# Three bf16 parts in place of one fp32 operand in the GRU aggregations of a two-layer graph kernel on one core

## The chip, the core and the metric

The kernel runs on one core of a Trainium2 chip. Five engines work side by side, each through its own queue strictly in the order in which the program lists its instructions: TensorE (PE in the profile, with its weight loads as PEld), VectorE (DVE), ScalarE (ACT), GpSimd (POOL) and SyncE (SP), which here issues all DMAs. Semaphores order the engines among each other. The metric is the device time of one execution in microseconds (us); the median of three runs is compared.

## The reference

128 graphs of 128 nodes with 256 features each, and an adjacency matrix per graph. Layer 0 is a gated graph network of three rounds, layer 1 a graph attention; both take a normalized input and add to it.

```python
h = jnp.maximum(_layernorm(x), 0.0)
A = (adj != 0).astype(x.dtype)
for i in range(3):                                  # layer 0: three GRU rounds
    m = jnp.einsum('bnd,de->bne', h, weight[i])
    aggr = jnp.einsum('bst,bsd->btd', A, m)
    h = _gru_cell(aggr, h, w_ih, w_hh, b_ih, b_hh)  # gates r, z, n
x = x + h
h = jnp.maximum(_layernorm(x), 0.0)                 # layer 1: attention
Wh = jnp.einsum('bnf,of->bno', h, W)
e = leaky_relu((Wh @ a1)[:, :, None] + (Wh @ a2)[:, None, :], 0.2)
att = softmax(where(adj == 0, -inf, e))             # 0 where adj == 0
x = x + jnp.einsum('bij,bjo->bio', att, Wh)
```

All inputs and outputs are fp32; A holds only 0 and 1.

## The kernel before

**Tiles.** Four graphs form a group; there are 32 groups. A group's state exists in two layouts: as columns (`hT`, features on the partitions, 2 chunks by 512 nodes) and as rows (`h`, nodes on the partitions, 4 graphs by 256 features). One *step* is one GRU round of one group, written (group, round); there are 96.

**A step** (`gru_step`). First the aggregation: `inputs` calls `gathered` (L637), which multiplies the rows `h` (the stationary operand, 128x128 per graph and chunk) by A, eight fp32 matmuls of 128 columns into two PSUM banks `pa`; ACT copies them to `aT` (L663), and DVE forms four sums of `aT` (`t_a`, L493, as it has formed `t_h` from `hT`). Then two blocks (`blocks`) of seven products each, a Strassen-like form of the gate matmuls (all at L737, three matmuls of 256 columns per product). Between the products stand evictions that the next product needs: ACT copies bank `u` to `c1_0` (L757) and bank `m7` to `m` (L760); DVE adds `u` and `m` into `c2` (L763), which must be done before the fifth product writes on into `u`; ACT copies `u` to `c1_1` (L770); DVE adds `u` and `m` into `c22` (L774). ACT does the tanh of the gates (L795, L802, L830, L688), DVE the updates: `candidate` (L682) and three passes over 1024 elements that make the new state (L694, L696, L698).

**Rows again.** For nearly every step the new columns become rows by DVE transposes of 32x32 blocks into `tq` and a trip through DRAM (`to_rows_by_blocks`, L590; four DMAs out, four back). Rows live in six buffers `h` (`ROWS = 6`), handed out in turn: rows of the state for a later step, the first rows of a group (`prologue`, `h_a`), and the rows of the attention layer (`epilogue`, `h_b`). A buffer comes free when the matmuls that read it are done.

**The epilogue** of a group, after its third round: rows by way of DRAM, `x1 + h` on DVE (L971), statistics (L440, L442, L446), a power on POOL (L454 to L458), normalization on ACT (L471), eight dot products on DVE (L998), one score vector transposed (L1026), written to DRAM and read back broadcast to all partitions (`line`, then `e`), Prelu on ACT (L1046), the mask `(A-1)*1e30` added on DVE (L930, L1055), row maximum (L1061), exponentials on ACT (L1065), a transpose by way of DRAM (L610), the attention matmuls `pq` (L637 again), `hs` copied by ACT (L1116), `po` (L1124) and the result (L1132).

**What sets the order.** A planner inside the kernel (class `Order`) runs when the program is built. It keeps, for every engine, the time at which it is free, and for every set of buffers ("room") when each comes free. Work beside the products is held in tasks (generators) that ask for an engine, a duration, a time from which they can start and sometimes a room; a task has a rank (0 for aggregation and sums, 0.5 for the new state, 1 for rows and prologue, 2 for the epilogue). `fill` hands out tasks of ACT and DVE while a product runs, the lower rank first when start times are close; `fixed` places an eviction; `finish` runs tasks until given ones are done, whatever PE does in that time. The order that results is fixed in the program, for every engine. The steps follow `plan`, sorted by 3*group + 4*round: in the middle of the run (22,2) is followed by (25,0), (24,1), (23,2) and (26,0). `settle`, called after every product, starts the inputs of the next step; if that step's rows are not yet planned, it calls `order.finish([s.rows])`.

```python
elif not groups[g].due:
    s = groups[g]
    s.due = True
    if s.l == l:
        if s.by_blocks():
            order.finish([s.rows])
        s.task = order.add(0, inputs(s, s.hT_ready))
```

Of the kernel before, what the change touches and what calls it, by code (L numbers as in the profile page):

```python
# [7 lines left out]

F32 = mybir.dt.float32
I32 = mybir.dt.int32  # L10
AF = mybir.ActivationFunctionType
ALU = mybir.AluOpType
AX = mybir.AxisListType

P = 128
D = 256
C = D // P
G = 4
T = G * P
# [8 lines left out]
def preln_gnn_kernel(  # L28
# [49 lines left out]

    ident = const.tile([P, P], F32, name="ident")
    make_identity(nc, ident)  # L80

# [14 lines left out]
            cols = slice(gates.start * D, gates.stop * D)  # L98
            dma(w[k][:, cols], weight[k * P : (k + 1) * P, cols])

    def load_weight(l, pool, shape, tag):
        w = borrowed(pool, shape, tag, f"wt_{l}", C * D)
        w = w.rearrange("p (c d) -> p c d", d=D)
        dma(w, weight_t[l].rearrange("(c p) d -> p c d", p=P))
        wt.append(w)


    load_weight(0, gate, [P, 2, H], "m")
    load_gates(wih, w_ih_t, slice(0, 1))
    xt_0 = io.tile([P, G, D], F32, tag="xt", name="xt_0", bufs=XT)  # L110
    for i in range(0, G, 2):
# [23 lines left out]

    zero = borrowed(gate, [P, C, T], "r", "zero", T, bufs=1).bitcast(mybir.dt.bfloat16)[:, 0:T]
    put(nc.vector.memset(zero, 0.0))
    c1 = [ps_sum.tile([P, 2, H], F32, name=f"c1_{n}") for n in range(2)]  # L140
    c2 = ps_sum.tile([P, 2, H], F32, name="c2")
# [31 lines left out]
    class Order:  # L173
        def __init__(self):
            self.free = dict.fromkeys((PE, ACT, DVE, POOL, SP, "port"), 0.0)
            self.tasks = []

            self.rooms = {room: [0.0] * 2 for room in ("tq", "x1", "prT", "e", "hs")}
            self.rooms |= {"misc": [0.0] * 3, "h": [0.0] * ROWS}
            self.next, self.room_of = dict.fromkeys(self.rooms, 0), {}  # L180

# [36 lines left out]
        def open(self, room, name):  # L218
            self.room_of[name] = room, self.next[room]
            self.next[room] = (self.next[room] + 1) % len(self.rooms[room])  # L220
            if room == "misc" and self.room_of[name][1] > 2:

                return more[self.room_of[name][1] - 3].rearrange("p n t -> p (n t)")
            if room == "misc":
                return ps_misc.tile([P, T], F32, tag="misc", name=name)
            if room == "h":
                return work.tile([P, G, D], F32, tag="h", name=name, bufs=ROWS)
            if room in ("prT", "e"):
                return work.tile([P, G, P], F32, tag=room, name=name)
            if room == "x1":  # L230
                return io.tile([P, G, D], F32, tag="x1", name=name, bufs=2)
            return work.tile([P, C, T], F32, tag=room, name=name)
# [411 lines left out]
            banks.append(pa)  # L644
        return banks, t

    def inputs(s, ready):

        name = f"{s.g}_{s.l}"
        s.tH, s.tA = {}, {}  # L650
        parts = len(s.parts())
        s.hidden = order.add(0, moving_sums(s.hT, s.tH, ready, f"h_{name}", parts))
        if s.l and not s.by_blocks():
            s.h, s.h_ready = yield from rows(s, ready, name)
        banks, ready = yield from gathered(s.h, s.A, s.h_ready, f"pa_{name}")
        order.close(f"h_{name}" if s.l else f"h_a{s.g}", ready)
        aT = None
        for c, pa in enumerate(banks):
            t = yield ACT, 0.57, ready
            order.close(f"pa_{name}_{c}", t)  # L660
            if aT is None:
                aT = columns_tile("aT", name)
            put(nc.scalar.copy(aT[:, c, :], pa))  # L663
        s.aT, s.aT_ready = aT, t
        yield from moving_sums(aT, s.tA, t, f"a_{name}", parts)

    def state_rows(s):
        s.h, s.h_ready = yield from to_rows_by_blocks(s.hT, s.hT_ready, f"{s.g}_{s.l}")

    def flat(tile_, cols):  # L670
        if cols == slice(0, T):
# [12 lines left out]
    def state(s, o, old, new, v, z, cols, graphs, halves, ready):  # L684

        n = v[:, o, cols]
        t = yield ACT, 0.66 if cols == slice(0, T) else 0.47, ready
        put(nc.scalar.activation(n, n, AF.Tanh, bias=bih[:, 2 * C + o : 2 * C + o + 1], scale=1.0))  # L688
        halves.append(t)
        if len(halves) < C:  # L690
            return
        n, new_, z_ = flat(v, cols), flat(new, cols), flat(z, cols)
        t = yield DVE2, both_t(cols), max(halves)
        put(nc.vector.tensor_tensor(new_, flat(old, cols), n, ALU.subtract))  # L694
        t = yield DVE2, both_t(cols), t - HOP
        put(nc.vector.scalar_tensor_tensor(new_, z_, 1.0, new_, ALU.add, ALU.mult))  # L696
        t = yield DVE2, both_t(cols), t - HOP
        put(nc.vector.scalar_tensor_tensor(new_, new_, 0.5, n, ALU.mult, ALU.add))  # L698
        if s.l < NL - 1:
            s.hT, s.aT = new, None  # L700
            s.l += 1
            s.hT_ready = t
            if s.by_blocks():
                s.rows = order.add(1, state_rows(s))
            if s.due:
                s.task = order.add(0, inputs(s, s.hT_ready))
        else:
            order.add((1.8 if s.g >= NG - 2 else 1.9 if s.g == NG - 3 else 2), epilogue(s, new, graphs, t))

    def gru_step(s, last, part):  # L710
# [38 lines left out]
        def blocks(no, gates):  # L749

            m = gate.tile([P, 2, H], F32, tag="m", name=f"m_{name}_{no}")
            c22 = gate.tile([P, 2, H], F32, tag="c22", name=f"c22_{name}_{no}")
            done = product(gates, lambda q: u[:, q, 0:W], W11, (0, 0), None, banks["u"], True, (ACT,))
            t = order.take(ACT, bank_t, max(done, banks["c1_0"]))
            put(nc.scalar.copy(c1[0][:, :, 0:W], u[:, :, 0:W]))  # L757
# [102 lines left out]
    class Group:  # L860


        def __init__(self, g):
            self.g, self.l, self.entered, self.aT = g, 0, False, None
            (self.xt, _), (self.at, self.at_ready) = xts.pop(g), ats.pop(g)
            self.scales = scales.pop(g)
            self.off_ready = 0.0
            self.kept, self.prT = [], None
            self.e = self.hs = None
            self.due = False  # L870

        def parts(self):


            return (0, 1) if self.g == NG - 1 and self.l == NL - 1 else (None,)

        def by_blocks(self):

            return places[self.g, self.l] - places[self.g, self.l - 1] > 2

    def load_x1(s):

# [22 lines left out]
    def prologue(s):  # L905

        g = s.g
        kept = []
        parts = s.scales if g == 0 else [s.scales]
        for i, (rstd, nb, t) in enumerate(parts):  # L910
            n = G // len(parts)
            graphs = range(i * n, i * n + n)
            s.h, t = yield from norm_apply(s.xt, graphs, rstd, nb, t, f"a{g}", kept)
        s.h_ready = t
        if g + XT < NG:
            order.add(1, load_task(load_rows, xts, g + XT, t))
        t2 = yield DVE, 0.36, s.at_ready
        s.A = work.tile([P, G, P], F32, tag="A", name=f"A_{g}", bufs=6)
        put(nc.vector.tensor_scalar(s.A, s.at, 0.0, None, ALU.not_equal))
        if g + AT < NG:  # L920
            order.add(1, load_task(load_adjacency, ats, g + AT, t2))
        transposed = to_columns if g < 2 else to_columns_by_blocks
        s.hT, s.hT_ready = yield from transposed(s.h, t, f"a{g}")
        if s.entered:
            s.task = order.add(0, inputs(s, s.hT_ready))

    def mask(s, ready):

# [11 lines left out]
    def epilogue(s, hT, graphs, ready):  # L940
# [46 lines left out]
        place = min(part.start, G - 2)  # L987
        for i in (1, 0):
            for k in graphs:
                first = not late and s.prT is None  # L990
                t = yield (DVE2, 0.53, ready, "prT") if first else (DVE2, 0.53, ready)
                if s.prT is None and late:
                    s.prT = io.tile([P, G, P], F32, tag="at", name=f"prT_{g}", bufs=AT)
                if s.prT is None:
                    s.prT = order.open("prT", f"prT_{g}")

                unused = s.prT[:, place : place + 2, :].rearrange("p k s -> p (k s)")
                put(nc.vector.scalar_tensor_tensor(  # L998
# [5 lines left out]
        if late:  # L1004
            t = yield PE, 4 * graph_t if end else graph_t, max(t, s.off_ready), "misc"
            p2 = order.open("misc", f"ps2_{name}")
            if end:

                put(nc.tensor.matmul(
                    p2[:, cols], ident, s.A[:, part, :].rearrange("p k s -> p (k s)"),  # L1010
                    start=True, stop=False, skip_group_check=True,
                ))
            for k in graphs:
# [86 lines left out]
        final = graphs[-1] + 1 == G  # L1100
        if final:
            order.close(f"h_b{g}_0", ready)
        if final and not end:
            order.close(f"e_{g}", ready)
        for c, pq in enumerate(banks):
# [66 lines left out]

    def settle(forced=False):

        if slot + 1 == len(plan):
            return
        g, l = plan[slot + 1]
# [5 lines left out]
# [3 lines that stand above are left out]
            if s.l == l:  # L1186
                if s.by_blocks():
                    order.finish([s.rows])
                s.task = order.add(0, inputs(s, s.hT_ready))

    def enter(forced):

# [7 lines left out]
            return None  # L1200
        s = waiting.pop(0)
        s.entered, s.state = True, [s.prologue]
        if s.prologue[2] is None:
            s.task = order.add(0, inputs(s, s.hT_ready))
        s.prologue[0] = 0
        order.tasks.sort(key=lambda t: t[0])
        admit()
# [27 lines left out]
    for slot, (g, l) in enumerate(plan):  # L1235
        s = groups[g]
        order.finish(s.state)
        settle()
        order.finish([s.task], lambda: s.aT is not None)
        order.free[PE] = max(order.free[PE], s.aT_ready + HOP)  # L1240
        s.due = False
# [48 lines left out]
```

## Time and profile before

| | |
|---|---|
| median of 3 runs | 2126.89 us (2126.03 to 2127.04) |
| span of the profiled execution, first to last instruction | 2124.5 us |
| PE busy (matmuls) | 2116.6 us |
| PE weight loads busy | 1886.8 us |
| DVE busy | 1733.1 us, 82% |
| ACT busy | 1301.4 us, 61% |
| POOL busy | 126.5 us |
| DMA engines, mean busy share on the main queue | 44.3% |
| matmul records at L637 for `pa` (1024 from `h`, 512 from `h_a`) | 124.7 + 62.4 us busy |

The profile gives no device time for the profiled execution itself beside its span; the median of the runs is 2.4 us above the span. Each fp32 matmul leaves two records. Matmul ends are modelled in the trace, so the distance between the starts of successive matmuls is read, not their length. "Idle before ... <- X" says how long an engine stood still before an instruction and what released it. Some records are followed by the next before their own end: the distance of starts is what an engine is occupied for.

### The profile page before, as it was taken

What the parts mean: (1) busy time and instruction counts of PE and PEld (TensorE: products, weight loads), DVE (VectorE), ACT (ScalarE), POOL (GpSimd) and SP (SyncE); (2) the same over time, 40 slices, a digit from 0 to 9 for tenths busy, and PEclk for the clock granted to TensorE, in tenths of its full rate; (3) what the DMA queues carried; (4) which work ended last, traced back from release to release, by engine and by line L of the source; (5) the groups of instructions that cost most, each with busy time, mean ns of one, the idle gap of its engine ahead of it and who ended that gap; (6) DMA issues with size and microseconds to landing.
All of it is one profiled execution on the core that took longest, in us unless ns stands there. A gap on an engine that the chain in (4) does not pass through costs nothing.

```text
span 2124.5 us, 32340 instructions
## 1 busy us (share of the span) xinstructions
PE 2116.6 (100%) x10865; PEld 1886.8 (89%) x10865; DVE 1733.1 (82%) x3771; ACT 1301.4 (61%) x2875; POOL 126.5 (6%) x200
## 2 busy tenths in 40 slices
PE   9999999999999999999999999999999999999999
PEld 7888888888888888888888888888888888888888
DVE  7778888888878888888888888888888888787777
ACT  5556666566656666666656666666666566665666
POOL 1000000000000000000000000000000000000000
PEclk9999999999999999999999999999999999999999
DMA  5334454554455444545344554445453544444311
GB/s 159 65 85 88 86 118 107 107 117 92 98 115 119 84 96 107 122 109 113 83 108 104 117 122 82 98 106 123 110 107 88 107 107 105 96 98 94 70 31 46
DMA packets 667975, 211.95 MB, mean 100 GB/s; under 512 B 578336, under 2 KB 644640, under 8 KB 667808
## 3 DMA queue, kind: packets, MB, share of 16 engines
q1 hardware_dynamic: 667808, 209.87, 44.3%
q8 instruction: 86, 1.41, 0.3%
q14 instruction: 81, 0.66, 0.1%
HBM read 121.91 MB, written 87.88 MB: 99 GB/s over the span
## 4 chain that ended last, share of the span: by engine, by line
PE 98%; DVE 1%; ACT 0%; DMA 0%; issue 0%; POOL 0%; SPq 0%; ACTq 0%; DVEq 0%
PE c L737 35%; PE u L737 35%; PE m L737 12%; PE pa L637 8%; PE po L1124 5%; PE pq L637 2%; PE pw L378 0%; DMA xt<-in_x 0%; PE c L1124 0%; PE u L1124 0%; ACT v L688 0%; PE c L637 0%; PE pr_o L527 0%; DVE st_a L440 0%; PE pr L527 0%; ACT e L1065 0%
## 5 line engine op out<-in xcount | busy, mean ns | idle before, releaser
L830 ACT ACTIVATE z<-c,brz 128x256 f32<-128x256 f32 (+1 forms) x388 | 186.2, 480 | 328.4 <-PE c L737 186.4
L737 PE MATMUL u<-t_h,s_hh 128*128 128x256 f32 (+1 forms) x1164 | 345.0, 378 | 0.9 <-DVE c L763 0.5
L737 PE MATMUL u<-t_a,s_f 128*128 128x256 f32 (+1 forms) x1164 | 312.3, 377 | 0.0
L737 PE MATMUL c<-aT,s_f 128*128 128x256 f32 (+1 forms) x1164 | 312.3, 377 | 0.0
L795 ACT ACTIVATE r<-c,brz 128x256 f32<-128x256 f32 (+1 forms) x388 | 175.3, 475 | 194.3 <-PE c L737 112.8
L763 DVE TENSOR_TENSOR c<-u,m 128x512 f32<-128x512 f32 (+1 forms) x194 | 134.6, 694 | 140.8 <-PE u L737 140.4
L737 PEld LDWEIGHTS u<-t_h,s_hh 128*128 128x128 f32 x1164 | 218.4, 190 | 31.3 <-ACT c L757 1.6
L737 PEld LDWEIGHTS c<-aT,s_f 128*128 128x128 f32 x1164 | 220.4, 190 | 28.9
L737 PEld LDWEIGHTS u<-t_a,s_f 128*128 128x128 f32 x1164 | 220.4, 190 | 29.0
L737 PE MATMUL c<-hT,s_hh 128*128 128x256 f32 (+1 forms) x780 | 229.8, 376 | 0.0
L837 DVE TENSOR_TENSOR v<-v,c 128x256 f32<-128x256 f32 (+1 forms) x388 | 153.6, 415 | 66.3 <-PE c L737 43.7
L770 ACT COPY c<-u 128x512 f32<-128x512 f32 (+1 forms) x194 | 109.7, 566 | 117.5 <-PE u L737 116.1
L760 ACT COPY m<-m 128x512 f32<-128x512 f32 (+1 forms) x194 | 112.7, 581 | 107.1 <-PE m L737 106.9
L802 ACT ACTIVATE v<-c,bhn 128x256 f32<-128x256 f32 (+1 forms) x388 | 173.0, 474 | 0.0
L737 PE MATMUL m<-t_h,s_hh 128*128 128x256 f32 (+1 forms) x582 | 172.3, 378 | 0.0
L737 PE MATMUL c<-t_h,s_hh 128*128 128x256 f32 (+1 forms) x582 | 172.1, 377 | 0.0
L737 PEld LDWEIGHTS c<-hT,s_hh 128*128 128x128 f32 x780 | 147.6, 190 | 19.2
L774 DVE TENSOR_TENSOR c<-u,m 128x512 f32<-128x512 f32 (+1 forms) x194 | 131.8, 679 | 37.9 <-ACT c L770 34.9
L737 PE MATMUL u<-aT,s_f 128*128 128x256 f32 (+1 forms) x582 | 156.2, 377 | 0.0
L737 PE MATMUL m<-t_a,s_f 128*128 128x256 f32 (+1 forms) x582 | 156.1, 377 | 0.0
L737 PE MATMUL c<-t_a,s_f 128*128 128x256 f32 (+1 forms) x582 | 156.1, 377 | 0.0
L757 ACT COPY c<-u 128x512 f32<-128x512 f32 (+1 forms) x194 | 109.8, 566 | 43.7 <-PE u L737 43.7
(164 smaller groups left out, 3928.4 us busy)
## 6 DMA issues: line engine op xcount, KB each, us to landing
z<-tq SPq DMA_DIRECT2D x248, 128.0 KB
h<-z SPq DMA_DIRECT2D x248, 128.0 KB
xt<-in_x SPq DMA_DIRECT2D x31, 512.0 KB
z_a<-tq_a SPq DMA_DIRECT2D x120, 128.0 KB
hT_a<-z_a SPq DMA_DIRECT2D x120, 128.0 KB
z_b<-tq_b SPq DMA_DIRECT2D x116, 128.0 KB
h_b<-z_b SPq DMA_DIRECT2D x116, 128.0 KB
x<-in_x SPq DMA_DIRECT2D x29, 512.0 KB
```

Of the source, the lines that this page charges most:

```text
L637: put(nc.tensor.matmul(pa[:, k * P : (k + 1) * P], h[:, k, c * P : (c + 1) * P], A[:, k, :], start=True, stop=True,))
L737: put(nc.tensor.matmul(to(q), S[0][:, gate_no, weight, :], moving, start=first and q == 0 and i == 0, stop=(i == len(ends) - 1), skip_grou ...
L757: put(nc.scalar.copy(c1[0][:, :, 0:W], u[:, :, 0:W]))
L760: put(nc.scalar.copy(m[:, :, 0:W], m7[:, :, 0:W]))
L763: put(nc.vector.tensor_tensor(c2[:, :, 0:W], u[:, :, 0:W], m[:, :, 0:W], ALU.add))
L770: put(nc.scalar.copy(c1[1][:, :, 0:W], u[:, :, 0:W]))
L774: put(nc.vector.tensor_tensor(c22[:, :, 0:W], u[:, :, 0:W], m[:, :, 0:W], ALU.add))
L795: put(nc.scalar.activation(r[:, o, cols], src, AF.Tanh, bias=brz[:, o : o + 1], scale=0.5))
L802: put(nc.scalar.activation(v[:, o, cols], src, AF.Identity, bias=bhn[:, o : o + 1], scale=0.5))
L830: put(nc.scalar.activation(z[:, o, cols], src, AF.Tanh, bias=brz[:, C + o : C + o + 1], scale=0.5))
L837: put(nc.vector.tensor_tensor(v[:, o, cols], v[:, o, cols], src, ALU.add))
L1124: put(nc.tensor.matmul(po[:, j, :], hs[:, c, k * P : (k + 1) * P], gwt[:, c, :], start=(c == 0), stop=(c == C - 1),))
```

## The change

A is kept in bf16 (0 and 1 are exact there). For the aggregation the rows `h` are split into three bf16 parts whose sum is the fp32 value: ACT rounds `h` to bf16 (`pair[:, 0]`), DVE subtracts it from `h` in place, ACT rounds the rest (`pair[:, 1]`), DVE subtracts again, and what is left has its value in the upper 16 bits of each fp32 word, which are read with a stride (`upper`). Each of the eight fp32 matmuls becomes three bf16 matmuls that accumulate. The splitting is a task of rank 0.5 that may start once the step is two places ahead in the plan and the rows are there. Four steps of the 96 (the first three of the plan and the last) keep the fp32 matmuls and get A copied to fp32. The tiles `parts` take SBUF, and `m` and `c22` go from two buffers to one. The planner gets rooms for `parts` and for the late `prT`. The matmul that adds the mask in the last two groups reads A and the identity as bf16.

```diff
+    def split(s):
+        name = f"{s.g}_{s.l}"
+        t = yield ACT, 1.2, s.h_ready, "parts"
+        pair = order.open("parts", f"parts_{name}")
+        for i in range(2):
+            if i:
+                t = yield ACT, 1.2, t
+            put(nc.scalar.copy(pair[:, i], s.h))
+            t = yield DVE2, 1.22, t
+            put(nc.vector.tensor_tensor(s.h, s.h, pair[:, i], ALU.subtract))
+        s.pair, s.pair_ready = pair, t
+        if s.hidden is not None:
+            s.task = order.add(0, inputs(s))
+    def gathered_by_parts(s, ready, name):
+        banks = []
+        t = yield PE, 0.17 * C * G, ready, "misc", C
+        for c in range(C):
+            pa = order.open("misc", f"{name}_{c}")
+            for k in range(G):
+                for i, part in enumerate((s.pair[:, 0], s.pair[:, 1], upper(s.h))):
+                    put(nc.tensor.matmul(
+                        pa[:, k * P : (k + 1) * P],
+                        part[:, k, c * P : (c + 1) * P],
+                        s.A[:, k, :],
+                        start=(i == 0),
+                        stop=(i == 2),
+                    ))
...
+    def allow_split(s, l):
+        s.early = l
+        if s.l == l and s.h_set:
+            s.split = order.add(0.5, split(s))
...
-        banks, ready = yield from gathered(s.h, s.A, s.h_ready, f"pa_{name}")
+        if s.whole():
+            banks, ready = yield from gathered_whole(s, s.h_ready, f"pa_{name}")
+        else:
+            banks, ready = yield from gathered_by_parts(s, s.pair_ready, f"pa_{name}")
+            order.close(f"parts_{name}", ready)
+            s.pair = None
...
-            m = gate.tile([P, 2, H], F32, tag="m", name=f"m_{name}_{no}")
-            c22 = gate.tile([P, 2, H], F32, tag="c22", name=f"c22_{name}_{no}")
+            m = gate.tile([P, 2, H], F32, tag="m", name=f"m_{name}_{no}", bufs=1)
+            c22 = gate.tile([P, 2, H], F32, tag="c22", name=f"c22_{name}_{no}", bufs=1)
...
-        s.A = work.tile([P, G, P], F32, tag="A", name=f"A_{g}", bufs=6)
+        s.A = work.tile([P, G, P], BF16, tag="A", name=f"A_{g}", bufs=6)
...
     def settle(forced=False):
+        if slot + 2 < len(plan):
+            g, l = plan[slot + 2]
+            s = groups.get(g) or next((w for w in waiting if w.g == g), None)
+            if s is not None and s.early != l and not s.whole(l):
+                allow_split(s, l)
...
-                s.task = order.add(0, inputs(s, s.hT_ready))
+                start_inputs(s)
...
+        if not s.whole():
+            order.finish([s.split])
         order.finish([s.task], lambda: s.aT is not None)
```

## The prediction

> **What bounds the kernel now.** I read the page's busy times and chain first, then one stretch of the timeline, then what DVE waits for.
>
> ```profile
> span 2124.5 us, 32340 instructions
> ...
> PE 2116.6 (100%) x10865; PEld 1886.8 (89%) x10865; DVE 1733.1 (82%) x3771; ACT 1301.4 (61%) x2875; POOL 126.5 (6%) x200
> ...
> PE 98%; DVE 1%; ACT 0%; DMA 0%; issue 0%; POOL 0%; SPq 0%; ACTq 0%; DVEq 0%
> PE c L737 35%; PE u L737 35%; PE m L737 12%; PE pa L637 8%; PE po L1124 5%; PE pq L637 2%; PE pw L378 0%; DMA xt<-in_x 0%; PE c L1124 0%; PE u L1124 0%; ACT v L688 0%; PE c L637 0%; PE pr_o L527 0%; DVE st_a L440 0%; PE pr L527 0%; ACT e L1065 0%
> ```
>
> PE is the bound throughout, and the aggregation `pa` is 8% of its chain. DVE, though, is next at 82%. The timeline around 1007 us shows the work that matters later:
>
> ```profile
> 1007.46 1.03 PE L737 MATMUL c<-aT,s_f 128*128 128x256 f32 x4
> ...
> 1008.52 0.42 DVE L837 TENSOR_TENSOR v<-v,c 128x256 f32<-128x256 f32 x1 [0.51 <-PE c L737]
> ...
> 1009.04 0.47 ACT L830 ACTIVATE z<-c,brz 128x256 f32<-128x256 f32 x1 [0.51 <-DVE v L837]
> ...
> 1009.62 1.95 PE L637 MATMUL pa<-A,h 128*128 128x128 f32 x16
> ...
> 1010.30 1.33 ACT L688 ACTIVATE v<-v,bih 128x512 f32<-128x512 f32 x2
> ...
> 1011.40 0.60 PE L737 MATMUL m<-t_h,s_hh 128*128 128x256 f32 x2
> 1011.48 0.35 SPq L60 DMA_DIRECT2D e<-line  x1
> ...
> 1011.67 1.23 DVE L694 TENSOR_TENSOR hT<-hT_a,v 128x1024 f32<-128x1024 f32 x1 [1.13 <-ACT v L688]
> ```
>
> One step's aggregation is 16 records from 1009.62 to the next start at 1011.40: 1.78 us, 0.111 a record. A product of three matmuls is 1.30 us (0.217 a record).
>
> ```profile
> L763 DVE TENSOR_TENSOR c<-u,m 128x512 f32<-128x512 f32 x190 | 132.9, 699 | 138.3 <-PE u L737 137.9
> L682 DVE SCALAR_TENSOR_TENSOR v<-r,v 128x1024 f32<-128x1024 f32 x95 | 116.1, 1222 | 20.8 <-ACT v L802 20.4
> ```
>
> Before each eviction `c2` (L763) DVE stands idle and waits for PE, 0.73 us on average: that is the spare time which keeps PE fed, and it is what the change spends.
>
> **The change on PE.** 92 of 96 steps get 24 bf16 matmuls of 128 columns for 8 fp32 ones. The trace has only three bf16 matmuls:
>
> ```profile
> 1.17 1.46 PE L146 MATMUL c<-zero 128*128 128x512 bf16 x3 [1.17 <-DVE zero L139]
> ```
>
> Successive starts are (1.46-0.63)/2 = 0.416 us apart for 512 columns, so 0.104 for 128: the upper end. But PE was slow then:
>
> ```profile
> 5.20 2.21 PEld L378 LDWEIGHTS pw<-wih,wt 128*128 128x128 f32 x6 [0.88 <-DMA wih<-in_w_ih_t]
> ```
>
> Those are records of 256 columns, 0.40 us apart against 0.217 later, although the granted clock reads 1.00 in both places. Scaled by 0.217/0.40 the bf16 matmul is 0.056, which is also half an fp32 record; this is the lower end and my value. Per step 24 x 0.056 = 1.34 against 1.78; over 92 steps **-40 us**. With 0.104 it would be 2.50 and +66 us.
>
> The Trainium skill (TensorE: Matmul & The Clock Gate, section "Back-to-back issue gap") speaks against the change: it gives about 81 ns per matmul for a sustained stream of weight load and matmul at 128 columns, and 56 ns only without the loads' share. By 81 ns, an estimate, a step would cost 1.94 and the change would lose 15 us on PE alone. No row here has such a stream in bf16.
>
> **The change on ACT and DVE.** Two ACT roundings per step: 1024 elements at about 1.15 us (the 512-element L688 averages 716 ns, and 256 more elements than L830's 482 ns cost 0.23), 184 x 1.15 = 212 us, so ACT goes from 1301 to about 1510 us. Two DVE passes over 1024 elements: records of 1.22 us whose successor starts 1.14 later (L696 to L774 at 1016.46 and 1017.60): 184 x 1.14 = 210 us. DVE: 1733 + 210 = 1943 of 2085 us, 93%. Since DVE's granules are 1.14 us and the evictions may not be late, whether that fits is a matter of order, and the order is fixed in the program. `m` and `c22` with one buffer cost nothing: `m` is last read by L774 after the fifth product and rewritten after the ninth, two products (2.6 us) of cover; without it, a product's 1.3 us per block.
>
> So I took the order of the changed program's instructions on each engine and added up DVE's occupancies (0.60 for 512 elements, 0.35 for 256, 0.66 for a 32x32 transpose, 0.54 for a dot product, 0.53 for statistics of one graph, 1.14 for 1024) between successive `c2` evictions, and PE's records between the same points. In the old order PE has more work than DVE in each of 190 intervals (the sum, 1738 us, fits the profile's 1733). In the new order DVE has more in 30 of them, 194 us in total, and nearly all of that is in 15 intervals. In those, **epilogue work that has been put off is placed between two steps**. Between (22,2) and (25,0), for instance, DVE has 25.4 us and PE 12.6, and ACT's order is (with the lines of the new file)
>
> ```
> L768  v_22_2   tanh of the new state     x2
> L1151 e_20     exponentials              x4
> L477  h_b21    normalization             x4  waits POOL
> L1132 e_21     Prelu                     x4  waits DMA
> L1151 e_21     exponentials              x4  waits DVE
> L1204 hs_20    <- pq_20                  x2  waits PE
> L837  c1_0     <- u of step (25,0)           waits PE
> ```
>
> PE can do `pq_20` and the first two products of (25,0), then the third needs that last copy. Why it is there: the rows of (24,1) need a buffer `h`, the next in turn is that of `h_b20`, two epilogues have not been finished for want of DVE time, and `order.finish([s.rows])` runs them with PE's work standing.
>
> **The length of one stretch**, from the end of (22,2)'s last product (1008.49 in the timeline's terms): L837, L830 and two tanh L688 end 2.3 later; three dependent passes 3 x 1.25, at 6.05; transpose 0.66, two `x1+h` 1.2, four statistics 2.2, L446 0.17, at 10.3. From L446 to L471:
>
> ```profile
> 2086.96 0.17 DVE L446 TENSOR_SCALAR norm_b<-mv_b 128x4 f32<-128x4 f32 x1
> ...
> 2088.84 2.08 ACT L471 ACTIVATE h_b<-xt,norm_b 128x256 f32<-128x256 f32 x4 [0.24 <-POOL norm_b L458]
> ```
>
> that is 1.7 from DVE's end to the first normalization, 0.5 for it, then eight dots and small ones 4.5 and the score transpose 0.2: 17.2. The four `line` DMAs are issued 0.4 later in 1.3, and `e` is issued 2.2 after them (the median of the run; 1009.02 to 1011.48 above): 21.1. When `e` lands is seen once, where ACT waited for it:
>
> ```profile
> 554.48 0.69 SPq L60 DMA_DIRECT2D e<-line  x1
> ...
> 559.95 0.40 ACT L1046 ACTIVATE e<-e,s 128x128 f32<-128x128 f32 x1 [0.90 <-DMA e<-line]
> ```
>
> 5.5 us: 26.6. Prelu 1.3, mask 0.67, maximum 0.68, exponentials 2.0, two `hs` 1.0, the copy of `u` 0.57: **32.9**. Of this PE works 1.78 + 2.60; it stands for **28.5 us**.
>
> By the same rows the other stretches that hold such a chain: (5,0) to (4,1) 28.5, (7,0) to (6,1) 29, (9,0) to (8,1) 25 (its normalization is done earlier), (14,0) to (13,1) 30 (four more normalizations), (14,2) to (17,0) 38 (the rows of group 17 go through DRAM behind it), (16,2) to (19,0) 31, then (18,2), (20,2), (22,2) and (24,2) with 28.5 each, (29,0) to (28,1) 24. Eleven, **320 us**. Four short ones, before (1,1), (12,0), (14,0) and (30,1), where a group's rows or parts come late: 28 us. The other 15 intervals with too much DVE work: 22 us less 0.4 of slack each, about 15.
>
> After each long stand PE may start slow, as at the start, where it was slow from 3.85 to about 7.5 us: 4 us at half speed, 2 us lost, 11 x 2 = 22 (between 0 and this; I take it, as the start is the nearest row). The skill's section "What's actually happening" on the same page says that the array falls to half its clock after an idle window of about 3.4 us and needs as much activity to come back; that agrees with the start, and the unmoved granted clock does not show it.
>
> **Sum**: 2124.5 - 40 + 320 + 28 + 15 + 22 = 2469.5 of span, 2.4 around it: about **2470 us** against the median 2126.9, 16% slower.
>
> **Rivals.**
> 1. *DVE's work alone counts* (0.11): the waits in the chain (POOL, the DMA landings) are shorter or lie beside DVE's other work, and a stretch costs only DVE's surplus over PE: 2126.9 - 40 + 194 = 2281. For it: that is all the sum of the order proves. Against it: ACT's list above, which waits in turn.
> 2. *bf16 matmuls at 0.104* (0.05): 2470 + 106 = 2576. For it: the only bf16 row. Against it: the fp32 records beside it are as slow.
> 3. *The stretches don't show, and the change is faster* (0.04): PE gets past them, because the scores of the epilogue are ready before the last product ends. Then only PE's saving is left, 2126.9 - 40 = 2087. It decides if the 15 stretches cost less than 40 us together, 2.7 each; the smallest of the eleven has 25.2 us of DVE work for 13.9 of PE, so this takes an error in my reading of the order.
>
> **How the numbers follow.** The forecast has 0.80. Its own range: with `e` landing in 2.5 us instead of 5.5 each chain is 3 shorter (-33), without slow starts -22, without the 15 small intervals -15, and with each long stretch 4 us shorter through overlap -44: 2356; with bf16 matmuls at the upper end 2576. Range 2350 to 2576, which leaves out rivals 1 and 3. Faster by over 0.2% 0.03, within 0.2% (about what a measurement of this kernel can tell) 0.01, slower 0.96.
>
> **What would show it.** Right: PE stands some 28 us about every 130 us, most of it before products that ACT's copy of `u` or a `pq` releases; in the same places DMA waits at Prelu; PE dense between them; 24 bf16 matmuls in about 1.35 us. Wrong: no stands over 5 us, or stands that DVE alone fills (rival 1), or a bf16 distance near 0.1.

## The result, and the profile after

The changed kernel takes 2515.74 us (median of four runs, 2513.07 to 2518.86) against 2126.85 (2126.03 to 2127.04) for the kernel before: a ratio of 1.183, 95% interval 1.1813 to 1.1846. The forecast was 2470 in a range of 2350 to 2576. So the sign and the range held, and the time is 46 us above the forecast. Further down, a kernel for which no interval is given was run once.

From the page of the changed kernel: span, busy times, TensorE's busy share and its granted clock in 40 slices, and the chain by engine.

```profile
span 2516.0 us, 34284 instructions
...
PE 2155.3 (86%) x11597; PEld 1879.3 (75%) x11598; DVE 1940.9 (77%) x3959; ACT 1485.6 (59%) x3059; POOL 129.1 (5%) x200
...
PE   9899789598799996898497696996969969869997
...
PEclk9999889799899998999699798998989989989998
...
PE 64%; DVE 10%; DMA 5%; SPq 4%; ACT 3%; issue 1%; POOL 0%; DVEq 0%; ACTq 0%
```

PE was 100% busy and is 86% busy now. The holes in its row come at regular distances, and the clock falls in the same slices. DVE has 208 us more work, but its share went down, from 82% to 77%: no engine is busy enough to be a bound over the whole span. PE's waits for other engines (line, what it waited for, us in total, times, longest):

```profile
PE pq L643 <- DMA e<-z_e: 184.0, 11, 25.8
PE u L817 <- ACT c L837: 69.3, 13, 24.4
PE pa L680 <- ACT parts L665: 37.8, 9, 21.5
```

The matmuls `pq` and `u` are those that the prediction named. The stretch between (22,2) and (25,0), for which it had worked out a chain, looks like this in the timelines of PE and of ACT; the last product of (22,2) ends at about 1857.8:

```profile
1876.15 3.75 PE L643 MATMUL pq<-e,h_b 128*128 128x128 f32 x16 [18.32 <-DMA e<-z_e]
...
1886.97 0.70 PE L817 MATMUL u<-t_h,s_hh 128*128 128x256 f32 x2 [3.73 <-ACT c L837]
```

```profile
1860.80 0.40 ACT L1151 ACTIVATE e<-e,soft 128x128 f32<-128x128 f32 x1 [0.71 <-DVE soft L1147]
...
1870.26 2.08 ACT L477 ACTIVATE h_b<-x,norm_b 128x256 f32<-128x256 f32 x4 [7.81 <-POOL norm_b L464]
1881.02 1.28 ACT L1132 ACTIVATE e<-e,s 128x128 f32<-128x128 f32 x4 [8.69 <-DMA e<-line]
1883.84 0.40 ACT L1151 ACTIVATE e<-e,soft 128x128 f32<-128x128 f32 x1 [1.54 <-DVE soft L1147]
...
1885.39 1.04 ACT L1204 COPY hs<-pq 128x512 f32<-128x512 f32 x2
1886.34 0.58 ACT L837 COPY c<-u 128x512 f32<-128x512 f32 x1
```

Line by line it is the list that the prediction read off the order of instructions: the exponentials of one epilogue, the next one's normalization, its Prelu behind a DMA, its exponentials, and last the copy of `u` that PE waits for. The engines take turns in waiting for each other; of the 29.1 us to the end of that copy PE works seven.

And the queue that carries the rows, SP's, around the same stretch:

```profile
1847.90 6.74 SPq L61 DMA_DIRECT2D z<-tq  x8
...
1877.79 0.35 SPq L61 DMA_DIRECT2D e<-line  x1
1886.26 2.57 SPq L61 DMA_DIRECT2D z_e<-prT  x4
1890.48 1.70 SPq L61 DMA_DIRECT2D e<-z_e  x4
1892.22 3.67 SPq L61 DMA_DIRECT2D h<-z  x8
```

The rows of two states are written to DRAM from 1847.90 on, and read back (`h<-z`) only 44 us later, right behind the second epilogue's `e<-z_e`. In the kernel before it takes 5 to 7 us around the same time, for instance:

```profile
1542.50 2.91 SPq L60 DMA_DIRECT2D z<-tq  x4
1548.09 1.71 SPq L60 DMA_DIRECT2D h<-z  x4
```

Over the whole run of the changed kernel, 24 of the 62 states' rows are read back more than 15 us after their writing began (79 at most); in the kernel before none takes over 11. This is the wait in `order.finish([s.rows])` that the prediction spoke of. What the rows wait for is the question of the experiments.

### The profile page after: what moved, and what is told of

Same layout as the page of the kernel before. It is cut to its first block, busy times and chain, and to the rows that moved or that the text cites. A ratio compares the mean times of both kernels' runs of the same rounds, so it can differ in the third digit from the quotient of the medians.

```text
span 2516.0 us, 34284 instructions
## 1 busy us (share of the span) xinstructions
PE 2155.3 (86%) x11597; PEld 1879.3 (75%) x11598; DVE 1940.9 (77%) x3959; ACT 1485.6 (59%) x3059; POOL 129.1 (5%) x200
## 3 DMA queue, kind: packets, MB, share of 16 engines
q8 instruction: 91, 1.49, 0.3%
## 4 chain that ended last, share of the span: by engine, by line
PE 64%; DVE 10%; DMA 5%; SPq 4%; ACT 3%; issue 1%; POOL 0%; DVEq 0%; ACTq 0%
PE u L817 24%; PE c L817 23%; PE m L817 8%; PE po L1212 4%; PE pa L680 4%; SPq L61 4%; DMA e<-line 2%; PE pq L643 2%; DVE prT L1084 1%; DVE hT L774 1%; DVE hT L776 1%; ACT e L1151 1%; DVE h L667 1%; DVE t_h L499 1%; DVE v L917 1%
## 5 line engine op out<-in xcount | busy, mean ns | idle before, releaser
L817 PE MATMUL u<-t_h,s_hh 128*128 128x256 f32 (+1 forms) x1164 | 354.5, 387 | 69.8 <-ACT c L837 69.3
L643 PE MATMUL pq<-e,h_b 128*128 128x128 f32 x464 | 75.3, 329 | 204.6 <-DMA e<-z_e 184.0
L643 PEld LDWEIGHTS pq<-e,h_b 128*128 128x128 f32 x464 | 71.7, 239 | 210.0 <-issue 187.9
L667 DVE TENSOR_TENSOR h<-h,parts 128x1024 f32<-128x1024 f32 x124 | 150.7, 1216 | 33.1 <-ACT parts L665 24.0
L850 ACT COPY c<-u 128x512 f32<-128x512 f32 (+1 forms) x194 | 110.2, 568 | 105.0 <-PE u L817 103.2
L680 PE MATMUL pa<-A,parts 128*128 128x128 bf16 x1472 | 139.7, 223 | 37.8 <-ACT parts L665 37.8
L762 DVE SCALAR_TENSOR_TENSOR v<-r,v 128x1024 f32<-128x1024 f32 (+1 forms) x97 | 117.5, 1212 | 69.3 <-ACT v L882 68.5
```

The costliest lines, as they stand in the source:

```text
L643: put(nc.tensor.matmul(pa[:, k * P : (k + 1) * P], h[:, k, c * P : (c + 1) * P], A[:, k, :], start=True, stop=True,))
L667: put(nc.vector.tensor_tensor(s.h, s.h, pair[:, i], ALU.subtract))
L680: put(nc.tensor.matmul(pa[:, k * P : (k + 1) * P], part[:, k, c * P : (c + 1) * P], s.A[:, k, :], start=(i == 0), stop=(i == 2),))
L762: put(nc.vector.scalar_tensor_tensor(v_, flat(r, cols), 1.0, v_, ALU.add, ALU.mult))
L817: put(nc.tensor.matmul(to(q), S[0][:, gate_no, weight, :], moving, start=first and q == 0 and i == 0, stop=(i == len(ends) - 1), skip_grou ...
```

## The experiments

Three theories. **Buffers in turn**: the six row buffers `h` are handed out strictly in turn. A late epilogue keeps one; when its turn comes again, the next state's rows wait for this one while others are free. The order that the program builds says so: when the rows of (24,1) are planned, `h_b20`, `h_b21` and `h_a26` hold a buffer each and three are free, but the next in turn is that of `h_b20`. **VectorE's time**, the prediction's reason: the 210 us added to DVE leave no room for the epilogues. **ScalarE**: the 1.05 us roundings take the epilogues' places on ACT. Beside these, the bf16 matmuls themselves could cost time that the stands cover.

Four runs with one part of the change taken out or altered. The first three leave out parts of the splitting, so they don't compute the same values.

**no_split**

```diff
 def split(s):
-    (two roundings on ACT, two subtractions on DVE)
+    pair, t = True, s.h_ready
...
 def gathered_by_parts(s, ready, name):
-    for i, part in enumerate((s.pair[:, 0], s.pair[:, 1], upper(s.h))):
+    for i, part in enumerate((upper(s.h), upper(s.h), upper(s.h))):
```

> The splitting is left out: no rounding on ScalarE, no subtraction on VectorE; the 24 bf16 matmuls all read the upper halves of h, so this computes with the upper halves alone. Buffers, ranks and the two-steps-ahead order stay. TensorE's records then sum to 2084 us (2123.8 less 92 steps at 0.44 us). If the cost of the change lies in the work of splitting, by whatever way, nothing is put off and the time is 2084 to 2105. If the bf16 matmuls themselves, or the clock they run at, cost something, it stays above 2150. If the earlier due times of the steps alone make the stands, it stays near 2500.

Measured: 2095.10 us, with PE 99% busy and a single wait over 3 us. The matmuls are not the trouble, and neither are the buffers alone: with nothing added no state's rows take over 10 us from writing to reading back, and the turn does no harm. `m` and `c22` have one buffer here too, so that cost next to nothing, as predicted.

**act_only**

```diff
             put(nc.scalar.copy(pair[:, i], s.h))
-            t = yield DVE2, 1.22, t
-            put(nc.vector.tensor_tensor(s.h, s.h, pair[:, i], ALU.subtract))
```

> Only the two roundings on ScalarE per step stay (124 of 1.05 us); the subtractions on VectorE are left out, so the three parts don't add up to h. VectorE's work is then that of before. The theory of the prediction (epilogues late for want of VectorE's time): no stretch without product, 2084 to 2120. The theory of the buffers (any added work ahead of the epilogues makes them late, and six row buffers handed out strictly in turn make the next state wait for a late epilogue's one while others are free): some ten stands of about 25 us stay, 2300 to 2380. A theory of ScalarE as the scarce engine gives the same as that of the buffers, and differs from it in the next two runs.

Measured: 2346.41 us. Busy times and PE's two largest waits in this run's profile:

```profile
PE 2135.7 (91%) x11597; PEld 1873.2 (80%) x11598; DVE 1728.5 (74%) x3775; ACT 1481.7 (63%) x3059; POOL 132.4 (6%) x200
```

```profile
PE u L815 <- ACT c L835: 104.2, 11, 13.8
PE pq L643 <- DMA e<-z_e: 80.9, 9, 22.3
```

The run has 184 such roundings, 124 of `h` and 60 of `h_a`. DVE has 1728.5 us of work, 5 less than in the kernel before, and PE stands at the same two places. 251 us come back over no_split without any work added to DVE: its time cannot be the whole reason.

**dve_only**

```diff
-            put(nc.scalar.copy(pair[:, i], s.h))
             t = yield DVE2, 1.22, t
-            put(nc.vector.tensor_tensor(s.h, s.h, pair[:, i], ALU.subtract))
+            put(nc.vector.tensor_tensor(s.h, s.h, upper(s.h), ALU.subtract))
...
-                for i, part in enumerate((s.pair[:, 0], s.pair[:, 1], upper(s.h))):
+                for i, part in enumerate((upper(s.h), upper(s.h), upper(s.h))):
```

> Only the two subtractions on VectorE per step stay (each takes the upper half of h off h in place; no rounding on ScalarE, no pair of bf16 tiles), so the parts don't add up to h. VectorE's time: about all of the cost stays, 2420 to 2520. ScalarE as the scarce engine: 2084 to 2130. The buffers: in the order of instructions twelve intervals hold more VectorE work than TensorE work, 133 us in sum where the changed kernel has 194 us; with its 432 us above TensorE's records scaled by this, about 300, so 2380 (2330 to 2450).

Measured: 2424.59 us, which rules out ScalarE as the only scarce engine, but lies in the ranges of the other two theories and doesn't part them. Either half of the splitting alone brings back most of the loss, 251 and 329 us over no_split, and both together 421: they don't add up, as a shared cause would have it.

**any_free**

```diff
 def begin(self, engine, ready, room=None, count=1):
+    if room == "h":
+        free = self.rooms["h"]
+        self.next["h"] = free.index(min(free))
...
 def open(self, room, name):
-    self.next[room] = (self.next[room] + 1) % len(self.rooms[room])
+    if room != "h":
+        self.next[room] = (self.next[room] + 1) % len(self.rooms[room])
...
-        return work.tile([P, G, D], F32, tag="h", name=name, bufs=ROWS)
+        return work.tile([P, G, D], F32, tag=f"h{self.room_of[name][1]}", name=name, bufs=1)
```

Each buffer gets a tag of its own, and weights that are loaded late into two of the row buffers name them by the new tags.

> All of the work and all of the parts stay; one thing differs from the changed kernel: a tile of rows gets whichever of the same six buffers comes free first, instead of the next in turn. The buffers: the stands before steps (g,1) and (g,2), which wait for a late epilogue's buffer, go; what stays are waits at the entry of a new group, as at most six groups are live (fourteen in the order, of 5 to 15 us of VectorE's work more than TensorE has): 2320 to 2400. VectorE's time or ScalarE's time: the work is the same and the time too, 2480 to 2520. If the buffers were all of it, 2090 to 2120.

Measured: 2357.89 us, 158 less with the same work and the same memory. The rows no longer wait; SP's timeline of this run, for one state:

```profile
1534.47 2.91 SPq L61 DMA_DIRECT2D z<-tq  x4
1541.55 1.94 SPq L61 DMA_DIRECT2D h<-z  x4
```

7 us from `z<-tq` to `h<-z` instead of 44, and none of the 62 takes over 9. But 274 us above PE's records are left, so the turn isn't all of it either. The next four runs ask what else.

**any_free_early**: any_free with the epilogue's rank changed.

```diff
-order.add((1.8 if s.g >= NG - 2 else 1.9 if s.g == NG - 3 else 2), epilogue(...))
+order.add((1.8 if s.g >= NG - 2 else 1.9 if s.g == NG - 3 else 1.2), epilogue(...))
```

> As any_free, and the epilogues have rank 1.2 instead of 2: they no longer stand behind the statistics and the scores of later groups, only behind the inputs, the splitting and the state's rows. Lateness of the epilogues as the root: the waits at the entry of new groups shrink, as the order's intervals with more VectorE work than TensorE work fall from 169 to 103 us in sum: 2358 less about half of its 274 us above TensorE's records, 2220 (2200 to 2300). VectorE's time as the root: rank changes only who waits, 2340 to 2370.

Measured: 2270.41 us, another 88 less. The epilogues were late also because they stood behind every other task.

**two_parts**: the changed kernel (buffers in turn, rank 2) with less splitting.

```diff
-    (two roundings on ACT, two subtractions on DVE)
+    t = yield DVE2, 1.22, s.h_ready, "parts"
+    pair = order.open("parts", f"parts_{name}")
+    put(nc.vector.tensor_tensor(pair[:, 1], s.h, upper(s.h), ALU.subtract))
...
-    for i, part in enumerate((s.pair[:, 0], s.pair[:, 1], upper(s.h))):
+    for i, part in enumerate((upper(s.h), s.pair[:, 1])):
```

> The changed kernel, with six buffers in turn and rank 2, but with h as two parts: its upper half as it lies, and the rest, which one VectorE subtraction writes as bf16; the rest is thus rounded. No rounding on ScalarE, one subtraction a step instead of two, 16 bf16 matmuls instead of 24: TensorE's records sum to 2043 us, VectorE has about 75 us more than in before instead of 216, ScalarE no more. VectorE's or ScalarE's time as the cause: a third of the cost or less, 2043 + 150, so 2190 at most. Buffers in turn: thirteen stands stay, each with 24 us of VectorE work beside 12.6 us of TensorE's, as long as those of the changed kernel (25 us and the slow clock after them, about 33): 2043 + 430, so 2470 (2420 to 2500).

Measured: 2402.65 us, a little below the range for the buffers in turn and 213 above the most that was expected of the other theories. That most was set too low: this kernel's DVE is busy 1834.6 us, 110 more than in no_split, which is half of the changed kernel's 216 and not a third; only ACT has nothing added. But half the cost would still be 2259 us, 144 under the measured time. Half of DVE's added work and none of ACT's costs nearly as much as all of it. PE waits 15 times for ACT's copy of `u`, 211 us.

**two_any_free**: two_parts with the buffers of any_free (and the tile of the parts cut to the half that is used).

> As two_parts, and a tile of rows gets whichever of the six buffers comes free first; nothing else differs. Buffers in turn as the main cause: most of the stands go; seven entries of groups stay with 4 to 12 us too much VectorE work: 2140 to 2220. If the buffers mattered only for any_free's heavier load, 2430 to 2480 as two_parts.

Measured: 2201.26 us, 201 less by the buffers alone, as the theory of the turn had it.

**two_any_seven**: two_any_free with rank 1.2 and seven live groups.

```diff
-LIVE = 6
+LIVE = 7
...
-s.A = work.tile([P, G, P], BF16, tag="A", name=f"A_{g}", bufs=6)
+s.A = work.tile([P, G, P], BF16, tag="A", name=f"A_{g}", bufs=7)
```

> As two_any_free, with epilogues at rank 1.2 and seven live groups (seven tiles of A) instead of six, so that a late epilogue doesn't hold up the entry of the next group. In the order no interval has over 3 us more VectorE work than TensorE work. The buffers and late epilogues as the whole cause: TensorE is the bound from end to end, 2043 + 2.4 and some small gaps: 2045 to 2075, faster than before by 2.5 to 3.9%. If the bf16 matmuls or the splitting have a cost of their own that the stands hid, 2100 or more.

Measured: 2095.60 us, ratio to before 0.9852 (0.9835 to 0.9868): 1.5% less time than before, but some 20 us above the range that was expected. Rank and groups were changed together, so their shares of the 106 us over two_any_free aren't known. In the profile, DVE's wait ahead of the subtraction (us, times), and PE's largest wait:

```profile
  DMA h<-z: 35.1, 26
```

```profile
PE u L816 <- DVE c L842: 19.3, 20, 2.2
```

The subtraction stands in DVE's order before the rows have landed; what is queued behind it is `c2` (L842), for which the fifth product waits. This wait is new: DVE's wait ahead of the subtraction is 0.7 us in two_parts and 8.0 in two_any_free, where PE stands for longer.

The last four runs: the missing corners, and this wait taken away.

**early_only**: the changed kernel with rank 1.2, buffers in turn.

> The changed kernel with the epilogues at rank 1.2 instead of 2 and the six row buffers in turn, as the changed kernel has them: the fourth corner beside any_free and any_free_early. Buffers in turn: a state's rows still wait for a late epilogue's buffer at ten places, each with 24 to 37 us of VectorE work beside 12.6 to 19 us of TensorE's: little is won, 2430 to 2510. If it is the rank alone that makes epilogues late, and the turn doesn't matter, about what any_free_early gives, 2250 to 2330.

Measured: 2484.88 us. Rank alone wins 31 us; with any free buffer it won 88.

**two_turn_seven**: two_any_seven with the buffers in turn.

> As two_any_seven, but with the six row buffers in turn, as the changed kernel has them; rank 1.2 and seven groups stay. Buffers in turn: nine stands come back before steps (g,1), each with 20.3 us of VectorE work beside 12.6 us of TensorE's; two_parts had 360 us above TensorE's records for thirteen stands, so 27.7 us each, here about 20 to 28 each: 2043 + 180 to 250 and the 50 us of two_any_seven's own: 2220 to 2330. If seven live groups and the rank were what helped, 2096 as two_any_seven.

Measured: 2324.55 us. The turn costs 229 us even with the lightest splitting, early epilogues and seven groups.

**two_landing**: two_any_seven, with the rows counted on later.

```diff
 def state_rows(s):
     s.h, s.h_ready = yield from to_rows_by_blocks(s.hT, s.hT_ready, f"{s.g}_{s.l}")
+    s.h_ready += 2.5
     rows_done(s)
```

> As two_any_seven, and the planner counts on a state's rows 2.5 us later, so that the subtraction isn't put into VectorE's order before they have landed. In two_any_seven VectorE stands 35.1 us in 26 waits for the rows' DMA ahead of the subtraction, and TensorE 19.1 us in some 24 waits of about 1 us for the copy of c that is queued behind it. If these waits are what is left above TensorE's records, 20 to 30 us go: 2066 to 2078. If VectorE's work in those steps is too much by itself, other work takes the place of the waits: 2088 to 2100.

Measured: 2060.27 us, ratio to before 0.9688 (0.9672 to 0.9704), 35 us less than two_any_seven and 6 below the range expected. Span and busy times:

```profile
span 2058.4 us, 32452 instructions
...
PE 2041.7 (99%) x10862; PEld 1799.6 (87%) x10862; DVE 1816.3 (88%) x3867; ACT 1308.7 (64%) x2875; POOL 125.4 (6%) x200
```

PE is the bound again, with DVE at 88%. This version is faster than both kernels, but its second part is rounded to bf16, so it is not the exact splitting of the change.

**three_landing**: the exact three parts in that arrangement.

> As two_landing (buffers by whichever is free, rank 1.2, seven groups, rows counted on later), but with the changed kernel's own three exact parts: two roundings on ScalarE, two subtractions on VectorE, 24 bf16 matmuls. If late epilogues and their buffers were the whole of the loss, TensorE's records (2084 us) and the 15 us that two_landing has above its own: 2100, faster than before by 1.2%. If the work of the splitting binds by itself once the waits for buffers are gone, any_free_early's 2270 less at most the 35 us that the later landing took off two_any_seven: 2220 to 2270, still slower than before.

Measured: 2255.98 us. With the waits for buffers gone, the work of the exact splitting still costs 196 us over two parts, of which 41 are matmuls.

All runs side by side. "Records" is an estimate of PE's busy time when nothing disturbs it, 2083.8 us with three parts and 2042.6 with two; where PE hardly stands, its busy time is 2081.5 (no_split) and 2041.7 (two_landing). "Stands" is PE's idle time in waits over 0.15 us; "slow" is PE's busy time less the records, for the most part the slow clock. The three add up to the span within 6 us.

| kernel | buffers | parts | rank, groups | us | records | stands | slow |
|---|---|---|---|---|---|---|---|
| changed | in turn | 3 | 2, 6 | 2515.7 | 2083.8 | 355.6 | 71.5 |
| no_split | in turn | none | 2, 6 | 2095.1 | 2083.8 | 8.2 | -2.3 |
| act_only | in turn | ACT's half | 2, 6 | 2346.4 | 2083.8 | 205.3 | 51.9 |
| dve_only | in turn | DVE's half | 2, 6 | 2424.6 | 2083.8 | 285.3 | 48.3 |
| early_only | in turn | 3 | 1.2, 6 | 2484.9 | 2083.8 | 328.2 | 67.1 |
| any_free | any | 3 | 2, 6 | 2357.9 | 2083.8 | 205.5 | 61.4 |
| any_free_early | any | 3 | 1.2, 6 | 2270.4 | 2083.8 | 140.5 | 40.3 |
| three_landing | any | 3 | 1.2, 7, later | 2256.0 | 2083.8 | 114.6 | 52.2 |
| two_parts | in turn | 2 | 2, 6 | 2402.7 | 2042.6 | 288.3 | 64.8 |
| two_any_free | any | 2 | 2, 6 | 2201.3 | 2042.6 | 123.0 | 29.8 |
| two_turn_seven | in turn | 2 | 1.2, 7 | 2324.6 | 2042.6 | 240.5 | 36.0 |
| two_any_seven | any | 2 | 1.2, 7 | 2095.6 | 2042.6 | 35.7 | 12.6 |
| two_landing | any | 2 | 1.2, 7, later | 2060.3 | 2042.6 | 13.0 | -0.9 |

Four pairs differ in the buffers alone: 158, 214, 201 and 229 us. Three pairs differ in the splitting (three parts or two): 113, 157 and 196 us. Both matter, and neither change alone gets below the kernel before. The traces show the turn itself in the same way: in the six kernels with buffers in turn and work added, 18 to 26 of the 62 states' rows are read back more than 15 us after their writing began; in the six with any buffer none takes over 11.

## Why the prediction was right, and where it was not

**The sum.** Predicted: 2084.5 of PE's records (2124.5 - 40), 363 of stands (320 + 28 + 15) and 22 of slow clock. Measured: 355.6 of stands, and a busy time of PE that is 71 us above those records where 22 were predicted. Of the 71, 59 are the slow clock: PE is busy for 118 us while the granted clock is 0.50. The rest is mostly the last record before a stand, which the trace shows some 0.16 us longer than the distance between starts, and there are 83 stands. The forecast is 46 us low, and the term that was mis-sized is the slow clock, 59 for 22.

**bf16 matmuls: right.** The timeline of PE at one aggregation of the changed kernel; 24 matmuls lie between the first start and that of the next product:

```profile
1039.01 0.27 PE L680 MATMUL pa<-A,parts 128*128 128x128 bf16 x2
...
1040.35 0.65 PE L817 MATMUL u<-t_h,s_hh 128*128 128x256 f32 x2
```

1.34 us, 0.056 each, as chosen; rival 2 (0.104) falls. The rule that spoke against the change, the Trainium skill's 81 ns per matmul for such a stream (TensorE: Matmul & The Clock Gate, "Back-to-back issue gap"), is not what these pairs of weight load and matmul show here. The prediction was right to put its one bf16 row down to a slow PE: the trace's record of the clock begins only 8.7 us into that run, so the 1.00 shown for the microseconds before isn't a reading.

**The long stretches: right in kind, not each in size.** Eleven, at the places named; PE stands 294 us in them (320 predicted). For the stretch worked out in full: first normalization 12.5 us after the last product (12.0 predicted), issue of `e` at 20.0 (21.1), Prelu at 23.2 (26.6), copy of `u` done at 29.1 (32.9). Most of the difference is one row: `e` was taken to land 5.5 us after its issue, and ACT starts here 3.2 us after it. That the stands in all were only 7 us off is in part luck: eight of the eleven were 40 us shorter together than predicted, three were 14 us longer (the one before (17,0) 44.2 us where 38 were predicted, the one before (19,0) 38.8 where 31 were), and all other stands come to 62 us, 43 predicted. Rival 1, DVE's surplus of work alone, falls: DVE stands still in these stretches too, 6.6 us at a time, as in the one at 1008 us:

```profile
1014.66 0.69 DVE L1141 TENSOR_TENSOR e<-e,A 128x512 f32<-128x512 f32 x1 [6.59 <-ACT e L1132]
```

**The slow clock: right in kind, little over a third of the size.** The prediction took one slow restart per long stretch and 2 us for it. The windows of the stretch at 1008 us in the changed kernel (length, then busy time of PE, PEld, DVE, ACT, POOL, the granted clock, DMA share, GB/s):

```profile
1008.40:1013.00 4.60, 4.57 (x19) 4.42 (x20) 0.00 (x0) 0.00 (x0) 0.00 (x0) 0.50 0.17 57
1013.00:1021.20 8.20, 2.89 (x11) 2.09 (x9) 4.03 (x9) 6.31 (x20) 0.00 (x0) 0.92 0.11 16
1021.20:1026.00 4.80, 4.73 (x15) 3.92 (x16) 2.11 (x5) 0.53 (x2) 0.00 (x0) 0.65 0.40 93
1026.00:1040.00 14.00, 14.00 (x87) 12.56 (x86) 6.82 (x10) 8.12 (x16) 0.00 (x0) 1.00 0.88 229
```

PE starts twice in a stretch, once for `pq` and once for the rest behind the copy of `u`, and it is slow both times: 4.6 us at 0.50 and 4.8 at 0.65 lose about 4 us, twice the price. The same goes for shorter stands that the sum gave no clock loss at all.

**"For want of DVE time": the step that failed.** The prediction had nearly all of the mechanism in its hands: the rows of (24,1) "need a buffer `h`, the next in turn is that of `h_b20`", and `order.finish` runs two epilogues with PE standing. It then put the lateness down to DVE. The runs show three conditions in its place. Something must make the epilogues late; ACT's roundings alone do (act_only, 251 us), with DVE's work as in the kernel before, and DVE's subtractions alone do (dve_only, 329 us). The rank of 2 keeps them late: 31 to 88 us. And the turn of the buffers makes the state wait for them: 158 to 229 us. The prediction didn't ask whether another buffer was free; three of the six were. The number came out nearly right all the same because it was read from the order of the program, which holds all three, and not from the reason given.

**What DVE's or ACT's time is worth** is at most what stays when the rows no longer wait for a buffer: 155 us in three_landing over two_landing beside the 41 of the matmuls. Whether one of the two engines binds there, or the length of the chain of four passes between a state's rows and its aggregation, wasn't tried; PE's largest wait in that run is for the second subtraction (32 us in 20 waits).

**Rival 3, the faster kernel**, needed that the stretches be hidden; its 2087 is about what no_split measures (2095). So the gain that the change aims at on PE is real. It is lost to the work of the splitting, and most of that loss to the order in which this work meets the epilogues: of the 421 us between the changed kernel and no_split, buffers, rank, groups and the later landing win back 260 (three_landing), and 161 stay with the exact parts.

## What to carry to other kernels

Where buffers are handed out in turn, one late user stops everyone behind it, however many are free: when a wait for a buffer shows up, ask whose turn it is before asking for more buffers or for less work. (Whether more buffers in turn would have helped here wasn't tried.) If work is added in front of a low-ranked chain that holds shared buffers, look at who waits for that chain, not only at the busy share of the engine that the work was added to. A stand of PE cost more than its length here, since the clock was slow behind it, 59 us beside 356 of stands: count the restarts, not the stretches.

## What the hardware showed that was not expected

Short waits were enough to halve PE's clock. In three_landing PE waits 1.54 us for the second subtraction and 0.39 us for `hs`, and is slow after that:

```profile
1135.43 0.23 PE L684 MATMUL pa<-A,h_a 128*128 128x128 bf16 x1 [1.54 <-DVE h_a L671]
...
1136.55 0.27 PE L684 MATMUL pa<-A,parts 128*128 128x128 bf16 x2 [0.39 <-ACT hs L1209]
...
1137.57 3.27 PE L1217 MATMUL po<-gwt,hs 128*128 128x256 f32 x8
1140.67 0.60 PE L822 MATMUL u<-hT_a,s_hh 128*128 128x256 f32 x2
```

Eight matmuls of `po` take 3.10 us from start to start instead of 1.73 (1000.12 to 1001.85 in the kernel before); `u` behind them is at full speed again. At 1068 us the same pattern is followed by three microseconds with a granted clock of 0.50, at 1204 us by none, and a single wait of 1.02 us in two_any_seven (628.90) by none.

What decides is seen in the clock itself. In these traces the granted clock changes only on a grid of 3.413 us. Here are the grid's steps around the three places in three_landing, each with the step behind it (columns as in the windows above):

```profile
1065.14:1068.56 3.42, 1.49 (x21) 1.09 (x19) 3.04 (x7) 2.60 (x6) 0.00 (x0) 1.00 0.93 142
1068.56:1071.97 3.41, 3.41 (x16) 2.87 (x13) 3.38 (x4) 2.08 (x4) 0.00 (x0) 0.50 0.42 119
1133.41:1136.82 3.41, 1.48 (x19) 1.07 (x18) 2.93 (x6) 2.53 (x6) 0.00 (x0) 1.00 0.92 141
1136.82:1140.24 3.42, 3.42 (x18) 2.88 (x15) 3.39 (x4) 2.18 (x4) 0.00 (x0) 0.50 0.49 126
1201.68:1205.09 3.41, 1.68 (x16) 1.20 (x15) 2.85 (x7) 2.50 (x5) 0.00 (x0) 1.00 0.80 122
1205.09:1208.51 3.42, 3.23 (x24) 2.94 (x24) 3.35 (x5) 2.69 (x5) 0.00 (x0) 1.00 0.46 114
```

Where PE is busy for 1.49 or 1.48 us of a step, the next step has half the clock; where it is busy for 1.68 us, the next has the full one. Counted over the 14 traces of this case: of the steps at full clock in which PE is busy for less than 0.40 of the time, all 174 are followed by half clock; between 0.40 and 0.50 it is 23 of 60, above 0.50 it is 2 of 8408. The way back asks for more: 190 of 191 half-clock steps with PE busy for 0.85 or more are followed by a full one, and 1 of 454 under 0.80. So it depends on where a wait falls on the grid as well as on its length. The Trainium skill (TensorE: Matmul & The Clock Gate, "What's actually happening") puts the slow state after an idle window of about 3.4 us that runs freely; the length of the window and its running freely agree with these traces, but here it need not be idle, since PE busy for less than about half of it was enough. Thus three_landing loses 39 us to the clock (78 us of PE's work at 0.50) with only six stands over 3 us.
